# A graph layer's edge attributes copied by group into spare columns of a PSUM tile, and a head in another order

## The chip, the cores and the metric

The kernel runs on one core of a Trainium2 chip. Its engines work side by side, each on its own list of instructions in a fixed order: PE (matrix products into PSUM), DVE (vector work), ACT (scalar functions and copies), POOL (which also issues the gathers) and SP (which only issues DMA). They wait for each other by semaphores. The metric is the device time of one launch in microseconds, the median of several runs. The inputs already lie in device memory.

## The reference

A graph of 1250 nodes with 512 features each (three vector parts of 128, and 128 scalars) and 40,000 edges, sorted by destination. Each edge has a source, a destination, an attribute of three numbers and a weight (its length). One message pass, an update that depends on nodes, a residual and a layer norm:

```python
x_j = x[src]
v_j = x_j[:, :384].reshape(E, 128, 3)
s_j = silu(x_j[:, 384:] @ W1 + b1) @ W3 + b3
edge_basis = rbf * cutoff @ W2 + b2
split = s_j * edge_basis
s1, s2, s3 = split[:, :128], split[:, 128:256], split[:, 256:]
v_msg = v_j * s1[:, :, None] + s3[:, :, None] * edge_attr1[:, None, :]
msg = concatenate([v_msg.reshape(E, 384), s2], axis=1)
x = x + segment_sum(msg, dst)
...
x = layernorm(x0 + x)
```

The left-out part gathers the new rows again, multiplies them with U and V, and adds a second segment sum; the kernel does that by node with counted links instead of by edge.

## The kernel before

**Head.** Everything is loaded, and for every node a row of a table is made: its vector part and `silu(s @ W1 + b1) @ W3 + b3`. `make_rows` does it by blocks of 128 nodes: a product on PE with the bias (L334) and W3 (L335), a copy on ACT (L593), a product on DVE (L594), a store by SP (L599). In between, the destinations `dst_r` become places within a window (`local_r`, L346 on POOL). Two reductions on DVE look for edges that lie outside their window; `misses` (L369) is summed by a one-column product on PE (`missed`, L378), copied to an integer, and decides a branch (L398). `by_tile` turns sources, weights and places into columns by PE transposes (L284). The attributes and places of all edges end up in one SBUF tile, `carried`, of shape 128 x groups x 16 tiles x 4: three attributes and the place. `sh.attr` and `sh.local` are views of it.

**Main loop.** 40,000 edges make 313 tiles of 128. A group g has 16 tiles and a batch t four of them, so t = 4g + i; there are 20 groups, the last one short. A step t of the loop issues, in this order:

- `messages(t)` on DVE: L916 and L918 multiply the gathered rows with the edge factors, which they read from the PSUM tile `eb` (four banks of 512 columns, a tile of edges in each, columns 0 to 383 used); then small work listed under `amid`; then `make_pair` (L939), and for the next batch `make_hot` (L847, a one-hot of the place within the window) and `make_spread` (L859, one-hot times each attribute);
- `add_messages(t-1)` on PE: L955 with the one-hot and L961 with the spread, into the sums by node;
- `count_links(t-1)` on PE: L984, preceded by L976 at a group's first batch;
- work listed under `early`, by step and rank, among it `bring_fades` (L809, a copy of 128x64 on ACT into spare columns of another PSUM tile), `make_basis` and `turn_basis` (L823 on PE, L828 on ACT);
- `edge_factors(t+1)`: L906, four products into `eb` for the next batch;
- `gather(t+3)`: four indirect DMAs on POOL (L756), the first of which also waits for the L906 just issued.

ACT makes a one-hot of sources in two lines, L871 (`distances`) and L881 (`mark_sources`), four instructions each a batch, and every other group a sine (L793). `eb` has a single buffer. Before the change L906 of a batch waits for L918 of the one before, the last that reads `eb`. The dependency is kept by tile: who writes any part of `eb` waits for whoever has read any part of it.

The last three batches use other PSUM tiles, and are not touched.

Of the kernel before, what the change touches and what calls it, by code (L numbers as in the profile page):

```python
# [22 lines left out]
C = 128  # L23
# [41 lines left out]
def gnn_resnorm(  # L65
# [89 lines left out]


    ones = const.tile([P, P], F32)
    nc.vector.memset(ones, 1.0)
# [7 lines left out]

    keep_warm(12)
    bias_f = front.tile([BIAS_ROWS - 1 + 32, V + 2 * C], F32, name="bias_f")
    nc.vector.memset(bias_f, 0.0)
    sh.nodes = const.tile([P, NB * width], F32, name="nodes")  # L170
    sh.xt = sh.nodes.rearrange("p (b f) -> p b f", f=width)
# [3 lines left out]

    inside = SHARE * (NCP - 1) - MARGIN
    assert all(0 <= inside - (SHARE * c - MARGIN) < WIN for c in range(full, NCP))
    dst_r = front.tile([NCP, CHUNK], I32, name="dst_r")
    nc.gpsimd.memset(dst_r[unfilled:, :], inside)
# [3 lines left out]
    nc.gpsimd.memset(sh.src_r[unfilled:, :], 0.0)  # L183

# [7 lines left out]
    def load_inner(engine, cols, b0):  # L192
        load_nodes(engine, sh, sh.xt, b0, min(b0 + 4, NB - 1), cols)
# [6 lines left out]
    load_inner(nc.scalar, of_s, 1)  # L200
    sh.w1_sb = load(nc.sync, w1, [C, C], "w1_sb")
    load_inner(nc.scalar, of_s, 5)
    nc.scalar.activation(warm, warm, AF.Silu)
    for b0 in (1, 5):
        load_inner(nc.gpsimd, slice(0, V), b0)
    load_outer(nc.gpsimd, slice(0, V))
# [139 lines left out]
    nc.gpsimd.tensor_scalar(local_r, dst_r, share, None, op0=ALU.subtract)  # L346
    nc.gpsimd.tensor_scalar(sh.src_r, sh.src_r.bitcast(I32), float(MARGIN), None, op0=ALU.add)
    for i in range(GROUP):
        nc.gpsimd.dma_start(w2_sb[i * FEAT : i * FEAT + N_RBF, :], w2)
        nc.gpsimd.dma_start(  # L350
            w2_sb[i * FEAT + N_RBF : i * FEAT + N_RBF + 1, :], b2.rearrange("(o f) -> o f", o=1)
        )
    ends = front.tile([NCP, 2], F32)
# [5 lines left out]
    inner_layer(next_s, (5, 6, 7, 8))  # L359
    load_edges(sh.wgt_r, edge_weight)  # L360
    make_rows((3, 4))
    nc.vector.tensor_reduce(ends[:, 0:1], local_r, AX.X, ALU.min)
    rest_s = turn_s((0, 9))
    make_rows((5,))
# [6 lines left out]
    )  # L371
    for h in range(2):
        nc.sync.dma_start(
            three[:, V + h * C : V + (h + 1) * C],
            bu2.rearrange("(h o c) -> h o c", o=1, c=C)[2 * h].to_broadcast([3, C]),
        )
    make_rows((7,))
    nc.tensor.matmul(missed, misses, ones[:NCP, 0:1], start=True, stop=True)  # L378
# [7 lines left out]
    part_bias(nc.gpsimd, slice(V, V + 2 * C))  # L386
    load_edges(sh.att_r, edge_attr, 3)
    sh.u_sb = load(nc.sync, u, [C, C], "u_sb")
    sh.v_sb = load(nc.sync, v, [C, C], "v_sb")
# [212 lines left out]
def windowed(tc, sh):  # L602
# [63 lines left out]
    with tc.tile_pool(  # L666
# [163 lines left out]
        def clear_rest(t, tile, engine=nc.vector):  # L830
            g, i = batches[t]
            for j in tiles(g, i):
                m = lanes(g, i, j)
                if m < P:
                    engine.memset(tile[m:, j], 0.0)

        def make_hot(t):
# [15 lines left out]

        def make_spread(t):
            g, i = batches[t]
            for js, n, m in runs(g, i):
                e = i * CPG + js.start
                shape = [m, n, 3, WIN]
                nc.vector.tensor_mul(  # L859
                    spread[t][:m, js],  # L860
                    hots[t][:m, js, None, :].to_broadcast(shape),
                    sh.attr[:m, g, e : e + n, :, None].to_broadcast(shape),
                )
# [1231 lines left out]
```

## Time and profile before

| | |
|---|---|
| runs shown | 568.67, 571.47, 572.39 us; median 571.47 |
| profiled execution | 567.24 us, its span 565.4 us |
| mean granted clock of PE | 0.907 |
| busy on the longest chain (page, part 4) | PE 55%, DVE 20%, ACT 13% |

An instruction's row gives start and duration in us, engine, line, operation, and the tiles it writes and reads. In brackets stands how long the engine was idle before it, and by the trace's inference what ended that. A row "x4" is four instructions in a run, with the time from the first start to the last end. The ends of PE's instructions are modelled. In a stretch's row stand, behind its bounds and length, the busy time of PE, PE's weight loads, DVE, ACT and POOL, then the granted clock of PE, the share of DMA and GB/s.

### The profile page before, as it was taken

To read this page: it belongs to the slowest core of one execution; us is meant where nothing else is said; L and a number is where in the kernel's file an instruction comes from. 1 tells how busy PE (TensorE), PEld (TensorE's weight loads), DVE (VectorE), ACT (ScalarE), POOL (GpSimd) and SP (SyncE) were. 2 spreads that over 40 slices of the span, in tenths; PEclk is the share of its full clock that TensorE was granted. 3 is DMA by queue.
4 is the path that set the end of the run, shared out by engine and by line. 5 is a ranking of instruction groups with operands and counts; after the bars stand their busy time and mean duration, and the time that the engine had idled before them with its cause. 6 is when DMAs were issued, how large, how long until landed. Compare 5 with 4: busy or idle time off the path is not lost.

```text
span 565.4 us, 11226 instructions
## 1 busy us (share of the span) xinstructions
PE 444.6 (79%) x4257; PEld 249.3 (44%) x4257; DVE 432.1 (76%) x660; ACT 377.0 (67%) x955; POOL 350.1 (62%) x377
## 2 busy tenths in 40 slices
PE   8557667677878787767887797879789698989993
PEld 6323233353344344435433443545445354445682
DVE  5576687778877877886778778787878887797675
ACT  3493565567777566775757687577768766788663
POOL 7775666666666666665556665666666666574530
PEclk9856998979897979988788897999989999999997
DMA  8786777777777776776777787678778777877413
GB/s 247 269 243 188 227 228 221 226 214 227 234 222 203 239 223 214 228 230 192 209 217 217 205 258 231 193 234 250 220 237 229 236 224 223 265 217 237 157 56 133
DMA packets 37938, 123.29 MB, mean 218 GB/s; under 512 B 7296, under 2 KB 9870, under 8 KB 37874
## 3 DMA queue, kind: packets, MB, share of 16 engines
q0 software_dynamic: 25824, 104.47, 62.6%
q1 hardware_dynamic: 10850, 17.35, 9.3%
q8 instruction: 35, 0.57, 0.4%
q10 hardware_dynamic: 1200, 0.66, 0.4%
q14 instruction: 29, 0.24, 0.2%
HBM read 112.94 MB, written 9.51 MB: 217 GB/s over the span
## 4 chain that ended last, share of the span: by engine, by line
PE 55%; DVE 20%; ACT 13%; issue 6%; another core or an unknown queue 3%; DMA 2%; POOL 0%; SPq 0%; DVEq 0%; POOLq 0%
PE eb L906 11%; PE agg L955 8%; PE agg L961 6%; DVE more L918 5%; PE adj L984 5%; PE begun L1359 5%; ACT one L881 5%; DVE nodes L918 4%; DVE more L916 3%; PE work L1146 3%; DVE nodes L916 3%; PE work L1051 2%; PE work L823 2%; ACT one L871 2%
## 5 line engine op out<-in xcount | busy, mean ns | idle before, releaser
L756 POOL DMA_INDIRECT more<-table,src_i x189 | 188.8, 999 | 106.2 <-issue 43.0
L756 POOL DMA_INDIRECT nodes<-table,src_i x124 | 123.5, 996 | 68.4 <-issue 28.6
L881 ACT ACTIVATE one<-one,weight,src_f 128x128 f16<-128x128 f16 x313 | 128.6, 483 | 0.2
L916 DVE TENSOR_TENSOR more<-more,eb 128x1024 f32<-128x1024 f32 (+2 forms) x48 | 57.2, 1193 | 63.8 <-PE eb L906 29.9
L871 ACT ACTIVATE one<-number,low 128x128 f16<-128x128 f16 x313 | 99.8, 393 | 6.9 <-remote 4.6
L906 PE MATMUL eb<-w_sb,basis_t 21*128 21x384 f32 x614 | 78.9, 577 | 29.4 <-DVE more L918 14.5
L918 DVE TENSOR_TENSOR more<-more,eb 128x1536 f32<-128x1536 f32 (+2 forms) x48 | 81.8, 1705 | 0.0
L916 DVE TENSOR_TENSOR nodes<-nodes,eb 128x1024 f32<-128x1024 f32 x30 | 36.6, 1222 | 39.4 <-PE eb L906 21.3
L955 PE MATMUL agg<-more,hot 128*32 128x512 f32 x378 | 61.7, 687 | 5.2 <-ACT sums L1006 5.2
L961 PEld LDWEIGHTS agg<-more,spread 128*32 128x32 f32 x1134 | 39.6, 119 | 37.8 <-issue 36.6
L984 PE MATMUL adj<-pair,one 128*128 128x160 f16 x313 | 38.0, 243 | 22.6 <-DVE basis L814 18.7
L918 DVE TENSOR_TENSOR nodes<-nodes,eb 128x1536 f32<-128x1536 f32 x30 | 52.4, 1747 | 0.0
L961 PE MATMUL agg<-more,spread 128*32 128x128 f32 x1134 | 48.6, 291 | 2.7 <-issue 2.7
L906 PEld LDWEIGHTS eb<-w_sb,basis_t 21*128 21x128 f32 x614 | 26.5, 198 | 51.9 <-issue 22.8
L859 DVE TENSOR_TENSOR spread<-hot,carried 128x384 f32<-128x384 f32 (+1 forms) x81 | 44.4, 549 | 2.7
L955 PE MATMUL agg<-nodes,hot 128*32 128x512 f32 x248 | 40.6, 658 | 3.9 <-ACT sums L1006 3.8
L984 PEld LDWEIGHTS <-one 128*128 128x128 f16 x313 | 23.4, 103 | 38.3 <-issue 36.4
L939 DVE TENSOR_TENSOR pair<-number,column 128x640 f16<-128x640 f16 (+1 forms) x81 | 38.7, 479 | 0.0
L961 PEld LDWEIGHTS agg<-nodes,spread 128*32 128x32 f32 x744 | 25.5, 118 | 23.1 <-issue 22.7
L961 PE MATMUL agg<-nodes,spread 128*32 128x128 f32 x744 | 31.8, 289 | 1.0 <-issue 0.9
L828 ACT COPY basis_t<-work 128x512 f32<-128x512 f32 x20 | 11.7, 587 | 29.6 <-PE adj L984 12.3
L1359 PE MATMUL begun<-upper,cast 128*128 128x512 f32 x57 | 28.1, 493 | 0.2 <-ACT cast L1350 0.2
(289 smaller groups left out, 711.2 us busy)
## 6 DMA issues: line engine op xcount, KB each, us to landing
table<-more SPq DMA_DIRECT2D x10, 320.0 KB
more<-table,src_i POOLq DMA_INDIRECT x189
spilled<-begun SPq DMA_DIRECT2D x10, 256.0 KB
more<-spilled SPq DMA_DIRECT2D x2, 1280.0 KB
node_x<-in_x_dram SPq DMA_DIRECT2D x35, 64.0 KB
nodes<-table,src_i POOLq DMA_INDIRECT x124
out_dram<-more SPq DMA_DIRECT2D x7, 256.0 KB
nodes<-in_x_dram POOLq DMA_DIRECT2D x2, 768.0 KB
```

The costliest lines, as they stand in the source:

```text
L756: got = nc.gpsimd.indirect_dma_start(out=rows_t[:n, j, :], out_offset=None, in_=sh.table1, in_offset=bass.IndirectOffsetOnAxis(ap=sh.src_i ...
L859: nc.vector.tensor_mul(spread[t][:m, js], hots[t][:m, js, None, :].to_broadcast(shape), sh.attr[:m, g, e : e + n, :, None].to_broadcast(sh ...
L871: nc.scalar.activation(onehots[t][:, j, :], number[:, :P], AF.Abs, bias=low[:, e : e + 1])
L881: nc.scalar.activation(one, one, AF.Relu, scale=less[:, e : e + 1], bias=worth[:, e : e + 1])
L906: made = nc.tensor.matmul(made_in[t][:, j, :V], turned[g][rows, i, :], sh.w2_sb[rows, :], start=True, stop=True,)
L916: nc.vector.tensor_mul(msg[:m, js, V:], msg[:m, js, V:], factors_of(t, js)[:m, :, C:V])
L918: nc.vector.tensor_mul(msg[:m, js, :V].rearrange("p t (k c) -> p t k c", k=3), msg[:m, js, :V].rearrange("p t (k c) -> p t k c", k=3), fac ...
L939: nc.vector.tensor_tensor(pair[:m, js, :].rearrange("p t (l h) -> p t l h", h=2), number[:m, : PARTS * WIN].rearrange("p (l h) -> p l h", ...
L955: nc.tensor.matmul(agg[j * WIN : (j + 1) * WIN, :], hots[t][:, j, :], msg[:, j, :width], start=(i == 0), stop=False, skip_group_check=True,)
L961: nc.tensor.matmul(agg[j * WIN : (j + 1) * WIN, c * C : (c + 1) * C], spread[t][:, j, c, :], msg[:, j, width:], start=False, stop=(i == la ...
L984: nc.tensor.matmul(to[:, :, at : at + WIN], one[:m, j, :], pair[:m, j, :].rearrange("e (p n) -> e p n", n=WIN), start=(i == 0 and j == js[ ...
L1359: nc.tensor.matmul(acc, casts[a, b], rows[:, a, :], start=(start and a == first and k == 0), stop=(stop and a == end - 1 and k == 1),)
```

## The change

1. `bring_carried(g)`, for the groups 1 to 18: one ACT copy of 128x64 from `carried` to columns 384 to 447 of bank g % 2 of `eb`. It is listed under `early` of step 4g - 3 behind `bring_fades`. `make_hot` and `make_spread` read the copy (groups 0 and 19 still `carried`).
2. In the head: six warming products instead of twelve; W3 is loaded second on SP; `dst` is loaded before SP's node loads; the fill of `dst_r` and the addition of a margin to the sources move from POOL to DVE; the eight loads of W2 and b2 move from POOL to SP, behind the attributes; two loads of bu2 and a bias part come earlier; the misses' product comes behind two more table rows.

```diff
-    keep_warm(12)
+    keep_warm(6)
...
+    sh.w3_sb = load(nc.sync, w3, [C, V], "w3_sb")
...
-    sh.w3_sb = load(nc.sync, w3, [C, V], "w3_sb")
+    load_edges(dst_r, dst)
     load_outer(nc.sync, of_s)
-    load_edges(dst_r, dst)
...
-    nc.gpsimd.tensor_scalar(sh.src_r, sh.src_r.bitcast(I32), float(MARGIN), None, op0=ALU.add)
-    for i in range(GROUP):
-        nc.gpsimd.dma_start(w2_sb[i * FEAT : i * FEAT + N_RBF, :], w2)
...
+    part_bias(nc.gpsimd, slice(V, V + 2 * C))
     make_rows((3, 4))
     nc.vector.tensor_reduce(ends[:, 0:1], local_r, AX.X, ALU.min)
+    nc.vector.tensor_scalar(sh.src_r, sh.src_r.bitcast(I32), float(MARGIN), None, op0=ALU.add)
...
-    make_rows((7,))
+    make_rows((7, 8, 0))
     nc.tensor.matmul(missed, misses, ones[:NCP, 0:1], start=True, stop=True)
-    make_rows((8,))
     nc.vector.tensor_copy(missed_i, missed)
-    make_rows((0, 9))
+    make_rows((9,))
...
     load_edges(sh.att_r, edge_attr, 3)
+    for i in range(GROUP):
+        nc.sync.dma_start(w2_sb[i * FEAT : i * FEAT + N_RBF, :], w2)
...
+        def bring_carried(g):
+
+            to = eb[:, g % 2, V : V + EPG * CARRY].rearrange("p (t k) -> p t k", k=CARRY)
+            nc.scalar.copy(to, sh.carried[:, g])
+            carried_at[g] = to
...
-                    sh.local[:m, g, e : e + n, None].to_broadcast(shape),
+                    carried_of(g)[:m, e : e + n, 3:].to_broadcast(shape),
...
-                    sh.attr[:m, g, e : e + n, :, None].to_broadcast(shape),
+                    carried_of(g)[:m, e : e + n, :3, None].to_broadcast(shape),
...
+        for g in range(1, NGR - 1):
+            at(early, 4 * g - 3, 6.5, bring_carried, g)
```

Line numbers shift: L906 becomes L917, L916 L927, L918 L929, L847 and L859 become L858 and L870, L871 and L881 become L882 and L892, L823 and L828 become L822 and L827, L955 and L961 become L966 and L972, L976 and L984 become L987 and L995. The copy is L841.

PE's rows around the factors of batch 14, before. A row is a line, an operation, the tiles written and read, and in brackets the engines or queues whose semaphores are waited for:

```order
L955 MATMUL agg<-more,hot 32x512 [waits DMASW1_49]
L961 MATMUL agg<-more,spread 32x128 x12
L823 MATMUL work<-ident,basis 128x128 [waits PE_49,Activation_49]
L823 MATMUL work<-ident,basis 128x128 x3
L906 MATMUL eb_403<-w_sb,basis_t 128x384 [waits DVE_49]
L906 MATMUL eb_403<-w_sb,basis_t 128x384 x3
L976 MATMUL adj<-passed,ident 128x5x16 [waits DVE_49]
```

And the same place with the change:

```order
L966 MATMUL agg<-more,hot 32x512 [waits DMASW1_49]
L972 MATMUL agg<-more,spread 32x128 x12
L822 MATMUL work<-ident,basis 128x128 [waits PE_49,Activation_49]
L822 MATMUL work<-ident,basis 128x128 x3
L917 MATMUL eb_397<-w_sb,basis_t 128x384 [waits Activation_49]
L917 MATMUL eb_397<-w_sb,basis_t 128x384 x3
L987 MATMUL adj<-passed,ident 128x5x16
```

The order stays; the factors' first product waited for DVE's L918 and now waits for ACT's copy. This is so for batches 4g - 2. The others wait for DVE as before, but there for `make_spread` (L870) instead of L918.

ACT at the same place, before:

```order
L871 ACTIVATE one<-number,low 128x128 x4
L828 COPY basis_t<-work 128x512 [waits PE_49]
L881 ACTIVATE one<-one,weight,src_f 128x128 [waits Activation_49] x4
L1176 ACT_TABLE_LOAD
L1176 ACTIVATE n_t<-work 128x128 [waits PE_49]
```

And with the change:

```order
L882 ACTIVATE one<-number,low 128x128 x4
L827 COPY basis_t<-work 128x512 [waits PE_49]
L892 ACTIVATE one<-one,weight,src_f 128x128 [waits Activation_49] x4
L841 COPY eb_397<-carried 128x64 [waits DVE_49]
L1187 ACT_TABLE_LOAD
L1187 ACTIVATE n_t<-work 128x128 [waits PE_49]
```

The copy stands behind the basis' copy and four one-hot instructions, and itself waits for DVE's `make_spread`. In the batches 10, 18, ... 66 it stands behind four L892, the sine (L792) and, every other time, `bring_fades` (L808).

PE in the head, where the misses' product moves (L378 before, L374 now), as a piece of the difference:

```order
-L378 MATMUL missed<-ones,misses 1x1 [waits DVE_49]
 L334 LDWEIGHTS ones_r
 L334 MATMUL pp<-bias,ones_r 128x384 [waits Activation_49]
 L335 MATMUL pp<-w_sb,h_t 128x384
 L334 LDWEIGHTS ones_r
-L334 MATMUL pp<-bias,ones_r 128x384
+L334 MATMUL pp<-bias,ones_r 128x384 [waits DVE_49]
 L335 MATMUL pp<-w_sb,h_t 128x384
+L374 MATMUL missed<-ones,misses 1x1 [waits DVE_49]
```

Two table rows that stood behind the product now stand ahead of it.

More of the change, by code (lines that the diff above doesn't have):

```diff
@@ L154, in load @@
         return t
+    inside = SHARE * (NCP - 1) - MARGIN
+    assert all(0 <= inside - (SHARE * c - MARGIN) < WIN for c in range(full, NCP))
     ones = const.tile([P, P], F32)
@@ L165, in keep_warm @@
             nc.tensor.matmul(idle[:, :P], ones, ones, start=True, stop=True)
-    keep_warm(12)
+    keep_warm(6)
     bias_f = front.tile([BIAS_ROWS - 1 + 32, V + 2 * C], F32, name="bias_f")
     nc.vector.memset(bias_f, 0.0)
+    dst_r = front.tile([NCP, CHUNK], I32, name="dst_r")
+    nc.vector.memset(dst_r[unfilled:, :], inside)
     sh.nodes = const.tile([P, NB * width], F32, name="nodes")
@@ L174, in gnn_resnorm @@
     nc.vector.memset(sh.xt[:MARGIN, 0, :], 0.0)
[L176 to L179, printed above, removed]
     diff = front.tile([P, P], I32)
@@ L205, in gnn_resnorm @@
         load_inner(nc.gpsimd, slice(0, V), b0)
+    nc.gpsimd.memset(sh.src_r[unfilled:, :], 0.0)
     load_outer(nc.gpsimd, slice(0, V))
@@ L360, in gnn_resnorm @@
     load_edges(sh.wgt_r, edge_weight)
+    for h in range(2):
+        nc.sync.dma_start(
+            three[:, V + h * C : V + (h + 1) * C],
+            bu2.rearrange("(h o c) -> h o c", o=1, c=C)[2 * h].to_broadcast([3, C]),
+        )
+    part_bias(nc.gpsimd, slice(V, V + 2 * C))
     make_rows((3, 4))
     nc.vector.tensor_reduce(ends[:, 0:1], local_r, AX.X, ALU.min)
+    nc.vector.tensor_scalar(sh.src_r, sh.src_r.bitcast(I32), float(MARGIN), None, op0=ALU.add)
     rest_s = turn_s((0, 9))
@@ L371, in gnn_resnorm @@
     )
[L372 to L376, printed above, removed]
-    make_rows((7,))
+    make_rows((7, 8, 0))
     nc.tensor.matmul(missed, misses, ones[:NCP, 0:1], start=True, stop=True)
-    make_rows((8,))
     nc.vector.tensor_copy(missed_i, missed)
-    make_rows((0, 9))
+    make_rows((9,))
     by_tile(ps_front, sh.src_r, 0, 1, sh.src_f, 1)
@@ L835, in clear_rest, with carried_of @@
                     engine.memset(tile[m:, j], 0.0)
+        carried_at = {}
+        def bring_carried(g):
+            to = eb[:, g % 2, V : V + EPG * CARRY].rearrange("p (t k) -> p t k", k=CARRY)
+            nc.scalar.copy(to, sh.carried[:, g])
+            carried_at[g] = to
+        def carried_of(g):
+            return carried_at.get(g, sh.carried[:, g])
         def make_hot(t):
```

8 lines of the change are left out of this document (3 added, 5 removed).

## The prediction

> **What bounds the kernel now.** I read the page's busy times and costliest groups first, then the timeline of PE, ACT, DVE and POOL around single batches, then the stretches by engine with the granted clock, and the head last. From the page, and from the answer on L756 in the loop (min/median/max in ns):
>
> ```profile
> PE 444.6 (79%) x4257; PEld 249.3 (44%) x4257; DVE 432.1 (76%) x660; ACT 377.0 (67%) x955; POOL 350.1 (62%) x377
> PEclk9856998979897979988788897999989999999997
> L859 DVE TENSOR_TENSOR spread<-hot,carried 128x384 f32<-128x384 f32 (+1 forms) x81 | 44.4, 549 | 2.7
> L756 POOL DMA_INDIRECT more<-table,src_i x189 | 188.8, 999 | 106.2 <-issue 43.0
> L756 POOL DMA_INDIRECT more<-table,src_i x166: 954/960/1296, 59.6 to 479.1; - x166
> ```
>
> No engine is full; the loop is a ring through PE and DVE. A batch t begins with L916 on DVE, which waits for the factors that PE's L906 writes into `eb`; L906 of the next batch in turn waits for L918, the last reader of `eb`. I call the start of L916 the beat. Three batches of the trace, t = 14, 38 and 34, by their timelines (start, duration). First t = 14:
>
> ```profile
> 123.89 0.93 PE L906 MATMUL eb<-w_sb,basis_t 21*128 21x384 f32 x8
> 120.30 1.75 DVE L918 TENSOR_TENSOR nodes<-nodes,eb 128x1536 f32<-128x1536 f32 x1
> 123.81 0.56 DVE L859 TENSOR_TENSOR spread<-hot,carried 128x384 f32<-128x384 f32 x1
> 125.28 1.22 DVE L916 TENSOR_TENSOR nodes<-nodes,eb 128x1024 f32<-128x1024 f32 x1 [0.91 <-PE eb L906]
> ```
>
> Then t = 38, with ACT first, PE, and DVE:
>
> ```profile
> 276.43 0.59 ACT L828 COPY basis_t<-work 128x512 f32<-128x512 f32 x1 [3.14 <-PE adj L984]
> 276.91 1.65 ACT L881 ACTIVATE one<-one,weight,src_f 128x128 f16<-128x128 f16 x4
> ...
> 272.81 0.66 PE L823 MATMUL work<-ident,basis 128*128 128x128 f32 x4
> 273.39 0.93 PE L906 MATMUL eb<-w_sb,basis_t 21*128 21x384 f32 x8
> 277.07 1.65 PE L1146 MATMUL work<-ident,square 128*128 128x128 f32 x6 [1.83 <-ACT basis_t L828]
> ...
> 271.58 1.75 DVE L918 TENSOR_TENSOR more<-more,eb 128x1536 f32<-128x1536 f32 x1
> 275.09 0.56 DVE L859 TENSOR_TENSOR spread<-hot,carried 128x384 f32<-128x384 f32 x1
> 276.52 1.22 DVE L916 TENSOR_TENSOR nodes<-nodes,eb 128x1024 f32<-128x1024 f32 x1 [0.87 <-PE adj L984]
> ```
>
> In t = 38 L918 ends at 273.33, L906 starts at 273.39, yet the beat comes at 276.52: 3.19 us after L918's end. In t = 14 L906 started 1.84 us after L918's end (122.05 to 123.89), and the beat came at 125.28, 3.23 us after it. So the beat doesn't follow L906's start one to one: a start up to about 1.9 us late costs nothing. PE still has earlier work in hand that the modelled ends don't show. In t = 38 ACT, too, gets the result of L823 (modelled end 273.47) only at 276.43.
>
> Last t = 34, ACT, PE, DVE:
>
> ```profile
> 247.37 1.63 ACT L881 ACTIVATE one<-one,weight,src_f 128x128 f16<-128x128 f16 x4
> 248.91 0.72 ACT L793 ACTIVATE turn<-turn 128x640 f32<-128x640 f32 x1
> 249.54 0.20 ACT L809 COPY adj<-fade 128x64 f32<-128x64 f32 x1
> ...
> 246.32 0.93 PE L906 MATMUL eb<-w_sb,basis_t 21*128 21x384 f32 x8
> 249.79 0.72 PE L976 MATMUL adj<-passed,ident 128*128 128x80 f32 x2 [2.54 <-ACT adj L809]
> ...
> 244.00 1.75 DVE L918 TENSOR_TENSOR nodes<-nodes,eb 128x1536 f32<-128x1536 f32 x1
> 248.98 1.22 DVE L916 TENSOR_TENSOR nodes<-nodes,eb 128x1024 f32<-128x1024 f32 x1 [0.40 <-remote]
> ```
>
> **The change, part by part.**
>
> *The new wait on DVE.* L906 (L917 now) waits for the one-hots' spread instead of for L918, since spread now reads a tile in the banks that PE writes. Spread ends at 275.65 in t = 38 and at 124.37 in t = 14, 2.3 us after L918; these two are among the batches with a turn on DVE ahead of it. In a plain batch it comes sooner, as at t = 40:
>
> ```profile
> 284.94 1.75 DVE L918 TENSOR_TENSOR nodes<-nodes,eb 128x1536 f32<-128x1536 f32 x1
> 287.33 0.56 DVE L859 TENSOR_TENSOR spread<-hot,carried 128x384 f32<-128x384 f32 x1
> ```
>
> There spread ends 1.2 us after L918 (286.69 to 287.89). The latest start, 2.3 after, plus 0.93 of L906 and 0.07 to the beat, ends 3.3 us after L918, where 3.2 is usual; the plain one ends at 2.2. I take 0; the cover is PE's unseen work. Without it, each of some 70 batches would lose at least those 1.2 us: bound +84, kept as a rival. Behind L917 on PE stand the sums of the messages, in front of nothing that DVE needs before the next beat.
>
> *The new wait on ACT.* Once in four batches, for t = 4g-2, PE's L917 waits for the copy of group g into `eb` (L841), and that copy stands behind the other work of its step in ACT's queue. Its price is near L809, the nearest row (128x64, 0.20 us, overlapping L793's end by 0.1). So it ends about 0.11 after the instruction ahead of it, and the beat comes 0.05 + 0.93 + 0.07 = 1.05 later.
> In t = 38 the last of four L881 ends at 278.56. Copy 278.67, beat 279.72 instead of 276.52: +3.2. PE's next pieces (L1146 at 277.07) stand behind L917 in its queue and move by as much, so this isn't won back. Eight batches (t = 14, 22, ... 70) look so; t = 6 is milder:
>
> ```profile
> 75.90 1.65 ACT L881 ACTIVATE one<-one,weight,src_f 128x128 f16<-128x128 f16 x4
> 76.17 1.22 DVE L916 TENSOR_TENSOR more<-more,eb 128x1024 f32<-128x1024 f32 x1 [0.75 <-PE adj L984]
> 476.68 1.66 ACT L881 ACTIVATE one<-one,weight,src_f 128x128 f16<-128x128 f16 x4
> 476.29 1.22 DVE L916 TENSOR_TENSOR more<-more,eb 128x1024 f32<-128x1024 f32 x1 [1.19 <-PE eb L906]
> 98.88 0.72 ACT L793 ACTIVATE turn<-turn 128x640 f32<-128x640 f32 x1
> 100.21 1.22 DVE L916 TENSOR_TENSOR more<-more,eb 128x1024 f32<-128x1024 f32 x1 [0.70 <-PE adj L984]
> ```
>
> By these rows t = 70, the last, gives 478.34 + 0.11 + 1.05 - 476.29 = +3.2; t = 6 gives 77.55 + 1.16 - 76.17 = +2.5; t = 10 gives 99.60 + 1.16 - 100.21 = +0.6. Sum of the nine: 8 x 3.2 + 2.5 = 28.1.
> In t = 34 the copy follows L809, which ends at 249.74: beat 250.90 instead of 248.98, +1.9. But there PE's L976 waited for L809 until 249.79 anyway and everything behind it goes on from there; now it starts when L917 ends, near 250.83. So only about 1.1 stays: four such batches (18, 34, 50, 66), 4.4. Three (26, 42, 58) have L793 but no L809, so nothing to give back: 1.8 each, 5.4. With t = 10: 10.4. For t = 2 I take nothing.
> The ends of this term: 28.1 + 10.4 = 38.5 as taken. Lower: L823's result reaches ACT in t = 38 at its modelled end, 3 us sooner, once L906 isn't pressed in behind it; then the copy waits for spread only and the nine batches cost 0.4 each, 14 in all. Upper: L906 costs 1.4 instead of 0.93 after such a wait, +8, 47.
>
> *PE's clock.* PE now idles in 17 places. Stretches by engine, from beat 37 to 38, 38 to 39, 39 to 40 (granted clock behind the busy times):
>
> ```profile
> 270.44:276.52 6.08, 4.61 (x56) 2.71 (x56) 5.17 (x7) 2.31 (x8) 4.10 (x4) 0.99 0.63 185
> 276.52:283.80 7.28, 6.73 (x51) 3.81 (x52) 4.84 (x7) 7.23 (x16) 3.84 (x4) 0.54 0.78 226
> 283.80:289.81 6.01, 5.32 (x70) 2.65 (x73) 4.85 (x7) 3.42 (x10) 3.84 (x4) 1.00 0.65 184
> ```
>
> A batch at half the clock takes 7.28 instead of 6.08 or 6.01: +1.2. The rows also show that a delay isn't made good: the next batch takes 6.01, not less. How many of the 17 places bring a new half-clock batch isn't shown: 0 to 17, so 0 to 20 us. I take 3, 4 us, since slices far below 0.8 are few in the row PEclk now.
> The Trainium skill, "TensorE: Matmul & The Clock Gate", section "HAM oscillation — how this bites in real kernels", says that gaps of PE above about 3.4 us throttle it again. By it the eight long waits, 273.47 to 278.72 on modelled ends, would each bring one: 10 instead of 4, and a sum 6 us higher. The trace only half agrees: its stretch at 0.54 follows a gap of 1.83 us.
>
> *Hot and spread with one operand in PSUM.* L859 costs 44.4 in all; a tenth either way is 4 us on DVE, which waits 0.4 to 1.2 us before each beat shown here. 0.
>
> *The head.* By its timelines:
>
> ```profile
> 14.74 1.57 POOL L346 TENSOR_SCALAR local_r<-dst_r,share 80x512 f32<-80x512 int32 x1 [2.97 <-DMA dst_r<-in_dst_dram]
> 16.19 0.81 PE L335 MATMUL pp<-w_sb,h_t 128*128 128x384 f32 x2
> 19.06 0.19 PE L378 MATMUL missed<-ones,misses 80*1 80x1 f32 x2 [2.07 <-DVE misses L369]
> 13.83 0.30 PE L297 MATMUL xs<-ident,nodes 128*128 128x128 f32 x1 [0.43 <-DMA counts<-in_edge_weight_dram]
> 3.03 1.61 SPq L428 DMA_DIRECT2D nodes<-in_x_dram  x4
> ```
>
> PE stands 2.07 us before the misses' product with three table rows behind it. With the product moved behind two of them that wait goes: at most -2.1. Against it SP issues w3 and dst ahead of the four node loads (1.61 us of issue from 3.03), so L297 at 13.83, which waits for such a load, may come up to 1.5 later. src_r's addition leaves POOL for DVE, which waits there; the eight w2 loads leave POOL for SP behind the attributes and have until L906 of batch 0. bu2's two loads go ahead of table stores on SP, and `part_bias` on POOL goes into what the w2 loads leave free. Fewer warming products: 0, since PE waits for loads behind them. I take -1; ends -2.1 and +1.5.
>
> Sum: 38.5 + 4 - 1 = +41.5. On the profiled run's own 567.24 (span 565.4) that is 608.7. The median of the runs shown, 571.47, lies 4.2 higher; I forecast against it: 613.
>
> **The rivals.**
>
> *ACT is early, the waits shrink.* The lower end above: 14 + 4 - 1 = +17, 588. For it: ACT idles 3.14 us before L828 in t = 38. Against it: it was released there 0.09 before the beat, by work of PE that comes before L906. Chance 0.14.
>
> *Every L917 is late.* If a start after spread moved the beat one to one, +84 on top: 697. t = 14 speaks against it. 0.06.
>
> *Faster: POOL sets the beat.* The gathers' mean is 999 against a minimum of 954 ns; over 313 that is 14 us. If the ring ran through POOL, one operand of hot and spread outside SBUF would give these 14 back, and L917's waits would fall into time in which DVE waits for rows anyway: 571 - 14 - 1 = 556. It decides only if POOL has no idle time, and the page has 106.2 before L756. 0.07. The Trainium skill, "SBUF — State Buffer", section "Who interferes with whom", has it that a DVE instruction with two inputs in SBUF contends with a GpSimd instruction that reads SBUF, and one with a single input doesn't; the spread from 954 to 1296 agrees with some such contention.
>
> *No change.* The copy's wait falls where PE is late anyway in nearly all 17 batches: within 566 to 577. Against it t = 34 and 38, where ACT ends after the beat. 0.07.
>
> **The numbers.** Chances: the forecast 0.66, with 595 to 640 as its own range; ACT early 0.14; all late 0.06; faster 0.07; none 0.07. Low 580 takes in most of the first rival; high 640 takes in 47 for the waits and 20 for the clock. Outside are the last three, 0.20. A measurement of this kernel tells about 1% from no change; slower by more than that: 0.66 + 0.14 + 0.06 = 0.86.
>
> **What would show it.** Right: L917 in every fourth batch released by ACT's L841, and beats 3 us longer there in t = 14, 22, ...; the other beats at about 6.05 (6.08 and 6.01 above). Wrong: L841 ending before the usual beat (ACT early); all beats longer than 7 (all late); beats under 6 (POOL). In the head, the product without a wait and the transposes behind the last table row about a microsecond sooner.

## The result and the profile after

The changed kernel takes 625.34 us in the median (623.36, 624.77, 625.9 and 633.58) against 571.93 for the kernel before (the three runs shown and a fourth, 573.67): 1.093 times as long, with a 95% interval of 1.0862 to 1.0997. This ratio leaves out the 633.58 as a slow run, and those of the experiments leave out runs over 1.5% above the fastest of their kernel. It is slower, inside the predicted range of 580 to 640 and 12 us above the predicted 613. The profiled execution took 623.36 us with a span of 621.5, which is 56.1 more than the span before; PE's mean granted clock fell from 0.907 to 0.861.

From the page of the changed kernel, busy times, the clock in 40 slices, and three of the costliest groups:

```profile
PE 463.2 (75%) x4245; PEld 258.2 (42%) x4245; DVE 432.0 (70%) x662; ACT 378.5 (61%) x973; POOL 330.9 (53%) x367
PEclk8956887878897797988878797979789977889998
L755 POOL DMA_INDIRECT more<-table,src_i x189 | 181.1, 958 | 146.0 <-PE eb L917 86.7
L917 PE MATMUL eb<-w_sb,basis_t 21*128 21x384 f32 x614 | 85.0, 618 | 95.0 <-ACT eb L841 46.9
L870 DVE TENSOR_TENSOR spread<-hot,eb 128x384 f32<-128x384 f32 x72 | 39.9, 554 | 2.5
```

DVE and ACT do as much as before (432.1 and 377.0 then), in a longer time. New is the last figure of L917's row: PE stood still for 46.9 us before the factors, until ACT's copy L841 had come. The gathers on POOL are shorter (958 instead of 999 ns), and wait longer, now mostly for those same factors.

Where the 56 us lie is told by the beats, the distances from one start of L916 (now L927) to the next. Summed over three kinds of batch, from the timelines of the two profiled executions:

| batches | before, us | after, us | difference |
|---|---|---|---|
| t = 6, 14, ... 70 (nine; basis product ahead) | 54.9 | 94.0 | +39.1 |
| t = 10, 18, ... 66 (eight; sine ahead) | 49.0 | 65.9 | +16.9 |
| the other 54 from t = 3 to 73 | 338.6 | 337.1 | -1.5 |
| start of the span up to the beat of t = 2 | 52.15 | 52.81 | +0.7 |

So 56.0 us came in the 17 batches whose factors wait for ACT's copy, and next to nothing elsewhere. Two executions of the same kernel can differ by some 3 us in such a row (below), so the last two differences aren't told from none. One of the nine, t = 14, by its timelines (ACT first, then PE, then DVE):

```profile
130.92 0.59 ACT L827 COPY basis_t<-work 128x512 f32<-128x512 f32 x1 [1.27 <-PE work L822]
131.40 1.65 ACT L892 ACTIVATE one<-one,weight,src_f 128x128 f16<-128x128 f16 x4
132.95 0.20 ACT L841 COPY eb<-carried 128x64 f32<-128x64 f32 x1
...
128.75 0.66 PE L822 MATMUL work<-ident,basis 128*128 128x128 f32 x4
133.21 1.66 PE L917 MATMUL eb<-w_sb,basis_t 21*128 21x384 f32 x8 [3.80 <-ACT eb L841]
...
125.87 1.75 DVE L929 TENSOR_TENSOR nodes<-nodes,eb 128x1536 f32<-128x1536 f32 x1
129.38 0.55 DVE L870 TENSOR_TENSOR spread<-hot,eb 128x384 f32<-128x384 f32 x1
135.00 1.22 DVE L927 TENSOR_TENSOR nodes<-nodes,eb 128x1024 f32<-128x1024 f32 x1 [5.06 <-PE eb L917]
```

The chain reads from the top: the basis's copy, four one-hot instructions, the small copy, and 0.06 us after its end PE's factors; the beat follows 0.13 us after those. DVE had been done with spread since 129.93 and stood 5.06 us. L917 took 1.66 us, where L906 took 0.93.

A batch with the sine and `bring_fades` ahead, t = 34, in the same order:

```profile
269.04 0.72 ACT L792 ACTIVATE turn<-turn 128x640 f32<-128x640 f32 x1
269.66 0.20 ACT L808 COPY adj<-fade 128x64 f32<-128x64 f32 x1
269.80 0.20 ACT L841 COPY eb<-carried 128x64 f32<-128x64 f32 x1
...
270.05 0.93 PE L917 MATMUL eb<-w_sb,basis_t 21*128 21x384 f32 x8 [2.92 <-ACT eb L841]
270.91 0.45 PE L987 MATMUL adj<-passed,ident 128*128 128x80 f32 x2
...
271.11 1.22 DVE L927 TENSOR_TENSOR nodes<-nodes,eb 128x1024 f32<-128x1024 f32 x1 [2.41 <-issue]
```

Here L917 kept its 0.93, and the beat of 8.12 us is 2.0 longer than before (6.12). Last a plain batch, t = 16, DVE ahead of PE:

```profile
142.30 1.75 DVE L929 TENSOR_TENSOR more<-more,eb 128x1536 f32<-128x1536 f32 x1
144.68 0.55 DVE L870 TENSOR_TENSOR spread<-hot,eb 128x384 f32<-128x384 f32 x1
147.27 1.22 DVE L927 TENSOR_TENSOR more<-more,eb 128x1024 f32<-128x1024 f32 x1 [1.22 <-PE work L1206]
...
145.29 0.93 PE L917 MATMUL eb<-w_sb,basis_t 21*128 21x384 f32 x8 [1.78 <-issue]
```

The factors start 1.24 us after L929's end (144.05), and the beat still comes 3.22 us after it, the distance of the kernel before.

### The profile page after: what moved, and what is told of

It is laid out like the page before. It is cut to its first block, busy times and chain, and to the rows that moved or that the text cites. A ratio compares the mean times of both kernels' runs of the same rounds, so it can differ in the third digit from the quotient of the medians.

```text
span 621.5 us, 11228 instructions
## 1 busy us (share of the span) xinstructions
PE 463.2 (75%) x4245; PEld 258.2 (42%) x4245; DVE 432.0 (70%) x662; ACT 378.5 (61%) x973; POOL 330.9 (53%) x367
## 4 chain that ended last, share of the span: by engine, by line
PE 55%; DVE 18%; ACT 14%; issue 6%; another core or an unknown queue 2%; SPq 0%; DMA 0%; POOL 0%; DVEq 0%; POOLq 0%; ACTq 0%
PE eb L917 16%; PE agg L966 9%; ACT one L892 6%; PE agg L972 5%; DVE more L929 5%; PE adj L995 4%; DVE more L927 4%; PE begun L1370 4%; DVE nodes L929 3%; PE work L1157 3%; DVE nodes L927 2%; PE work L822 2%; ACT one L882 2%; PE work L1062 2%
## 5 line engine op out<-in xcount | busy, mean ns | idle before, releaser
L755 POOL DMA_INDIRECT more<-table,src_i x189 | 181.1, 958 | 146.0 <-PE eb L917 86.7
L755 POOL DMA_INDIRECT nodes<-table,src_i x124 | 118.5, 956 | 96.8 <-PE eb L917 55.5
L917 PE MATMUL eb<-w_sb,basis_t 21*128 21x384 f32 x614 | 85.0, 618 | 95.0 <-ACT eb L841 46.9
L892 ACT ACTIVATE one<-one,weight,src_f 128x128 f16<-128x128 f16 x313 | 128.5, 482 | 0.2
L927 DVE TENSOR_TENSOR more<-more,eb 128x1024 f32<-128x1024 f32 (+2 forms) x48 | 57.2, 1193 | 102.0 <-PE eb L917 75.4
L882 ACT ACTIVATE one<-number,low 128x128 f16<-128x128 f16 x313 | 99.8, 392 | 24.5 <-PE adj L995 17.4
L929 DVE TENSOR_TENSOR more<-more,eb 128x1536 f32<-128x1536 f32 (+2 forms) x48 | 81.8, 1705 | 0.0
L927 DVE TENSOR_TENSOR nodes<-nodes,eb 128x1024 f32<-128x1024 f32 x30 | 36.6, 1221 | 58.2 <-PE eb L917 38.8
L917 PEld LDWEIGHTS eb<-w_sb,basis_t 21*128 21x128 f32 x614 | 27.4, 205 | 117.4 <-ACT eb L841 50.7
L966 PE MATMUL agg<-more,hot 128*32 128x512 f32 x378 | 66.3, 725 | 1.0 <-ACT sums L1017 0.6
L972 PEld LDWEIGHTS agg<-more,spread 128*32 128x32 f32 x1134 | 41.4, 123 | 35.4 <-issue 34.1
L929 DVE TENSOR_TENSOR nodes<-nodes,eb 128x1536 f32<-128x1536 f32 x30 | 52.4, 1747 | 0.0
L995 PE MATMUL adj<-pair,one 128*128 128x160 f16 x313 | 39.4, 252 | 16.9 <-DVE basis L813 16.9
L972 PE MATMUL agg<-more,spread 128*32 128x128 f32 x1134 | 49.3, 299 | 0.0
L966 PE MATMUL agg<-nodes,hot 128*32 128x512 f32 x248 | 41.9, 711 | 0.9 <-ACT sums L1017 0.6
L870 DVE TENSOR_TENSOR spread<-hot,eb 128x384 f32<-128x384 f32 x72 | 39.9, 554 | 2.5
L995 PEld LDWEIGHTS <-one 128*128 128x128 f16 x313 | 25.7, 109 | 33.8 <-issue 33.2
L972 PEld LDWEIGHTS agg<-nodes,spread 128*32 128x32 f32 x744 | 26.2, 121 | 23.4 <-issue 22.5
L972 PE MATMUL agg<-nodes,spread 128*32 128x128 f32 x744 | 31.2, 294 | 0.0
L1370 PE MATMUL begun<-upper,cast 128*128 128x512 f32 x57 | 30.1, 529 | 0.0
L1062 PE MATMUL work<-sums,sel 128*128 128x512 f32 x36 | 29.3, 939 | 0.2
```

Of the source, the lines that this page charges most:

```text
L755: got = nc.gpsimd.indirect_dma_start(out=rows_t[:n, j, :], out_offset=None, in_=sh.table1, in_offset=bass.IndirectOffsetOnAxis(ap=sh.src_i ...
L870: nc.vector.tensor_mul(spread[t][:m, js], hots[t][:m, js, None, :].to_broadcast(shape), carried_of(g)[:m, e : e + n, :3, None].to_broadcas ...
L882: nc.scalar.activation(onehots[t][:, j, :], number[:, :P], AF.Abs, bias=low[:, e : e + 1])
L892: nc.scalar.activation(one, one, AF.Relu, scale=less[:, e : e + 1], bias=worth[:, e : e + 1])
L917: made = nc.tensor.matmul(made_in[t][:, j, :V], turned[g][rows, i, :], sh.w2_sb[rows, :], start=True, stop=True,)
L927: nc.vector.tensor_mul(msg[:m, js, V:], msg[:m, js, V:], factors_of(t, js)[:m, :, C:V])
```

## Experiments

The theories. **A**, mine: the copy, late in ACT's queue, holds PE's L917 in 17 batches. Against it: L917's later start behind spread costs in every batch; the slow factors come from PE's clock after its pauses (**D**); the head loses time because the rows' bias (b3) arrives behind W3's load (**F**); or the reads and writes in PSUM themselves cost (**B**, together with the wait for spread). The experiments fell on four chips. On two of them the kernel before takes 567 to 571 us, as in the result; on the other two 494 to 496. So each ratio is against the kernel before on the same chip.

Beats of all profiled executions, summed as in the table above, with the median of the 54 others. Each row is one execution; two rows of one kernel show the scatter:

| kernel | nine, us | eight, us | 54 others, us | median |
|---|---|---|---|---|
| before | 54.9 | 49.0 | 338.6 | 6.10 |
| before, another chip | 57.8 | 49.9 | 338.4 | 6.19 |
| after | 94.0 | 65.9 | 337.1 | 6.17 |
| change of the loop alone | 91.4 | 66.4 | 335.0 | 6.09 |
| change of the head alone | 56.0 | 51.6 | 332.7 | 6.11 |
| copy first in its step | 65.3 | 52.5 | 338.4 | 6.09 |
| copy first, another chip | 65.3 | 50.6 | 343.3 | 6.17 |
| copy into SBUF | 56.7 | 51.7 | 335.6 | 6.11 |
| *faster chips:* before | 48.9 | 45.5 | 278.1 | 4.99 |
| W3 behind b3, loop as after | 67.4 | 55.0 | 301.5 | 5.43 |
| copy made, unread | 65.4 | 49.4 | 290.6 | 5.01 |
| copy made, unread, another chip | 63.4 | 49.3 | 290.4 | 5.02 |
| copy by DVE | 61.1 | 47.6 | 295.2 | 5.33 |
| PE kept at work | 61.4 | 51.0 | 291.5 | 5.13 |

**The loop alone and the head alone.** The first adds `bring_carried`, `carried_of` and the schedule's line to the kernel before; the second takes them out of the changed one.

```diff
 # main_only, on the kernel before
-                    sh.local[:m, g, e : e + n, None].to_broadcast(shape),
+                    carried_of(g)[:m, e : e + n, 3:].to_broadcast(shape),
...
+            at(early, 4 * g - 3, 6.5, bring_carried, g)
 # head_only, on the changed kernel
...
-            at(early, 4 * g - 3, 6.5, bring_carried, g)
```

> The kernel before with the copies of the main loop alone; the head is as before. Theory A (PE waits in every fourth batch for a copy that stands late in ACT's queue): the main loop carries nearly everything, 618 to 630 us, with beats of about 10.2 us at t = 14, 22, 30 and 8.1 at t = 18, 34. Rival H (a part comes from the head, whose table rows begin 3.5 us later in the changed kernel): under 616 us.

> The changed head alone, without copies. Theory A: within 1% of the kernel before, 568 to 577 us: the table rows begin 3.5 us later, end 0.9 later, and the main loop is as before. Rival H: 580 us or more.

Measured: 617.43 and 568.05 us against 566.63, which is 1.09 (1.0827 to 1.0973) and 1.0019 (0.9975 to 1.0063). The first lies just under A's 618 to 630, with the beats as expected. The loop's part carries all of it, the head nothing that can be told from no change.

**The copy first in its step.** The same copy, from ACT, ahead of the basis's copy and the one-hots.

```diff
-            at(early, 4 * g - 3, 6.5, bring_carried, g)
+            at(early, 4 * g - 3, -2, bring_carried, g)
```

> The changed kernel, but the copy is issued first among the work of its step, so on ACT it stands ahead of the basis' copy and the four one-hot instructions. It writes the same place and PE waits for it as before. Theory A: 576 to 590 us; the beats of the batches 4g-2 fall from 10.2 and 8.1 to 6.1 to 7.2 us. Rival B (what costs is that L917 waits for spread at all, or that DVE reads the attributes from PSUM): it stays above 610 us.

Measured: 576.28 us, 1.0163 (1.0096 to 1.0231). Some four fifths of the loss are gone: 9.7 us are left (576.28 - 566.63) of the loop's 50.8. (The profiled execution, which the table shows, was its longest, 583.29.) Twelve of the 17 beats lie at 6.1 to 7.2 us as expected; t = 6, 26, 54, 62 and 70 take 7.35 to 8.19. Batch 14 by its timelines, ACT, PE, DVE:

```profile
126.83 0.22 ACT L841 COPY eb<-carried 128x64 f32<-128x64 f32 x1 [1.09 <-DVE spread L870]
127.68 0.59 ACT L827 COPY basis_t<-work 128x512 f32<-128x512 f32 x1 [0.64 <-PE work L822]
...
126.75 0.89 PE L822 MATMUL work<-ident,basis 128*128 128x128 f32 x4
127.57 0.93 PE L917 MATMUL eb<-w_sb,basis_t 21*128 21x384 f32 x8
...
126.24 0.56 DVE L870 TENSOR_TENSOR spread<-hot,eb 128x384 f32<-128x384 f32 x1
128.62 1.22 DVE L927 TENSOR_TENSOR nodes<-nodes,eb 128x1024 f32<-128x1024 f32 x1 [1.83 <-PE eb L917]
```

The copy now waits for spread alone and is done at 127.05, half a microsecond before L917, which no longer stands. A second run on the other of these two chips, where the kernel before takes 570.81, scattered: 576.11 in one run and 585.75 to 587.53 in three, too wide for an interval; how much of the loss is left there stays open. The ratio on a faster chip, which this run was also to tell, wasn't measured.

> The same kernel as copy_first. Theory P: on a chip where the kernel before takes about 567 us, 1.01 to 1.025 times as long as before, as then; on a chip where it takes about 494 us, 1.04 to 1.07 times, since nothing of PE covers the wait for spread there. Rival Q: the same ratio on both.

**The copy into SBUF.** As many ACT copies at the same place, into a tile of its own.

```diff
-            to = eb[:, g % 2, V : V + EPG * CARRY].rearrange("p (t k) -> p t k", k=CARRY)
+            to = pool.tile([P, EPG, CARRY], F32, name="carried_g", bufs=2)
```

> The changed kernel, but the copy goes to an SBUF tile of its own (two buffers) at the same place in ACT's queue, so that PE waits neither for it nor for spread. Theory A: 568 to 577 us. Rival C (18 more instructions on ACT push its other work back): 590 us or more.

Measured: 568.69 us, 0.9995 (0.9945 to 1.0046). The copy's time on ACT costs nothing; its place in `eb`, with the waits of PE for the copy and for spread that come with it, costs everything. Its page also shows the gathers on POOL when both operands of hot and spread are in SBUF again:

```profile
L755 POOL DMA_INDIRECT more<-table,src_i x189 | 186.9, 989 | 107.9 <-issue 42.7
```

The gathers are back at 989 ns, where the changed kernel has 958 and the kernel with the copy first, which also reads PSUM, 959. The changed head alone has 988, so a part of the 41 ns came with the head.

**Copies made and not read; the copy by DVE.** The first leaves the one-hots and spread on `carried`, so L917 waits for the copy and for L929, but for no spread. The second puts the copy first and gives it to DVE.

```diff
 # unread
...
-                    carried_of(g)[:m, e : e + n, :3, None].to_broadcast(shape),
+                    sh.attr[:m, g, e : e + n, :, None].to_broadcast(shape),
 # copy_dve, beside rank -2
-            nc.scalar.copy(to, sh.carried[:, g])
+            nc.vector.tensor_copy(to, sh.carried[:, g])
```

> The changed kernel with its copies, but nobody reads them: hot and spread read SBUF as before. PE still waits for the copy in the batches 4g-2, and for L929 instead of spread in the others. Theory A (the queue on ACT): 612 to 628 us, the beats at t = 14, 22, 30 stay near 10.2 and those at 18, 34 near 8.1; against the changed kernel only the other beats shrink, by 0.05 to 0.1 us each, 3 to 5 us in all. Rival B (the wait for spread or the reads from PSUM cost): under 605 us.

> The changed kernel, but DVE makes the copy itself, right behind spread; PE waits for DVE alone. Theory A: 567 to 580 us, the beats of the batches 4g-2 under 7 us, since the copy is done 0.2 us after spread. Rival B: above 600 us, since all batches wait for spread and the reads from PSUM stay.

Measured, on a chip where the kernel before takes 494.27: 524.14 us, 1.051 (1.0427 to 1.0593), and 527.21, 1.0634 (1.0544 to 1.0724). The unread copy was run once more, on the other fast chip: 524.34 against 495.85, 1.061 (1.0511 to 1.071).

> The same kernel as unread, whose copies nobody reads. On a chip where the kernel before takes about 567 us, theory A: 1.08 to 1.10 times before, 612 to 626 us, beats near 10.2 at t = 14, 22, 30 and 8.1 at 18, 34, since only the wait for ACT is left; rival B (the wait for spread or the reads from PSUM cost a good part): under 1.06. On a chip where before takes about 494 us: 1.04 to 1.06 as in the first run of it.

The copy's wait alone, with nothing read from it, costs 16.5 us in the nine batches (65.4 against 48.9; the second run, on the same chip as that 48.9, has 63.4, or 14.5 more), which is A again. With the copy by DVE ACT is out of it, and yet 12.2 us remain in the nine: the copy stands behind spread on DVE, and L917 behind the copy. The expected times were worked out from the slower chips. Put as ratios to 566.63, A's ranges (1.08 to 1.11 for the unread copy, 1.00 to 1.02 for the copy by DVE) miss both, and the second run of the unread copy lies just above its 1.04 to 1.06. With the unread copy it is A's own price that is lower on these chips (see the rivals below). The copy by DVE lies in B's range (over 1.06): it costs 32.9 us without ACT. And with everything read, as in the changed kernel, the one execution below took 543.36, some 19 more than the unread copy. So on the faster chips A isn't the whole: the wait for spread or the reads from PSUM cost there too, and which of the two isn't shown.

**PE kept at work, and W3 behind b3.** The first puts two products that nobody reads ahead of L917 in the batches 6, 14, ... 70, so that PE's pause is shorter. The second is the changed kernel with W3's load behind b3's; its loop is that of the changed kernel, and stands for it on this chip, with one execution only.

```diff
 # stay_warm
+        def stay_warm():
+            idle = work()
+            for _ in range(2):
+                nc.tensor.matmul(idle[:, :V], ident, sh.w2_sb, start=True, stop=True)
...
+        for g in range(2, NGR - 1, 2):
+            at(early, 4 * g - 3, 6.6, stay_warm)
 # w3_behind
-    sh.w3_sb = load(nc.sync, w3, [C, V], "w3_sb")
...
     nc.sync.dma_start(three[:, :V], b3.rearrange("(o f) -> o f", o=1).to_broadcast([3, V]))
+    sh.w3_sb = load(nc.sync, w3, [C, V], "w3_sb")
```

> The changed kernel with two idle products of 384 columns on PE ahead of L917 in the batches 8k+6, into the basis' PSUM tile; their result is not read. Theory D (L917 takes 1.66 instead of 0.93 us there because PE has stood idle and got half the clock): L917 falls to about 0.93, the nine beats from 10.2 to 9.5, 6 us in all, 615 to 621. Rival E (the length of L917 there has another cause, or so short a stretch of work doesn't bring the clock back): L917 stays at 1.66 and the time at 622 to 630.

> The changed kernel with W3 loaded behind b3 again. Theory F (b3's bias comes late because W3's load went ahead of it): the first table row begins near 9.5 instead of 12.3 us and the transposes behind the last row 1 to 3 us sooner than 23.7. Rival G (the small b3 load is slow for other reasons, dst and the node loads): still above 11.5 us. The whole time is the same within 1% of the changed kernel.

Measured: 526.93 us for the first, 1.0654 (1.0577 to 1.0731), and 543.36 in a single run for the second, both against 494.27. Batch 14 with PE kept at work, ACT and then PE:

```profile
115.67 0.57 ACT L827 COPY basis_t<-work 128x512 f32<-128x512 f32 x1
117.68 0.22 ACT L846 COPY eb<-carried 128x64 f32<-128x64 f32 x1
...
114.88 0.66 PE L822 MATMUL work<-ident,basis 128*128 128x128 f32 x4
116.30 1.56 PE L839 MATMUL work<-w_sb,ident 128*128 128x384 f32 x4 [0.76 <-ACT basis_t L827]
117.95 0.93 PE L922 MATMUL eb<-w_sb,basis_t 21*128 21x384 f32 x8
```

And the same batch's factors, with W3 behind b3:

```profile
116.22 1.60 PE L917 MATMUL eb<-w_sb,basis_t 21*128 21x384 f32 x8 [2.42 <-ACT eb L841]
```

Both start 2.66 us after L929's end, so the copy's wait is the same; but after the two idle products the factors take 0.93 us, in this and the other eight batches, without them 1.60 here and 0.97 to 1.67 in the others. In the beats of the loop (t = 0 to 73) the idle products save 19.9 us: 6.0 in the nine batches, 4.0 in the eight, 10.0 in the others, head apart. The 6.0 is what D had named; what the idle products do for the batches that have none isn't shown, and the 19.9 is one execution against one. So D holds for the nine, on top of A: the pause that the copy makes also costs clock, though not always in L917. The unread copy has the same pause before batch 14, and there L917 keeps 0.93, while products behind it are slow: eight L966 take 1.63 us, and 1.06 with PE kept at work (L971 there).

```profile
113.63 0.93 PE L917 MATMUL eb<-w_sb,basis_t 21*128 21x384 f32 x8 [2.42 <-ACT eb L841]
116.89 1.63 PE L966 MATMUL agg<-nodes,hot 128*32 128x512 f32 x8
```

With PE kept at work the wait remains, and the kernel stays behind the one before.

For F the first bias product of the table, and the first transpose behind the table, with W3 behind b3:

```profile
10.73 0.48 PE L334 MATMUL pp<-bias,ones_r 65*128 65x384 bf16 x1 [3.09 <-DVE bias L321]
...
22.14 0.44 PE L284 MATMUL tp<-ident,counts 80*128 80x80 f32 x4
```

With PE kept at work, on the same chip and with W3 ahead, they stand at 12.66 and 25.01. F is right in direction, 1.9 and 2.9 us, but W3's place is the small part of b3's delay. In the kernel before SP issues b3's load at 1.71 us, and DVE's first use of it, L316, starts at 4.94. The changed kernel has 2.15 and 8.70. With W3 behind b3 the issue is at 1.71 again, and still:

```profile
7.97 0.44 DVE L316 CAST bias<-bias_f 65x384 bf16<-65x384 f32 x1 [2.56 <-DMA bias_f<-in_L_gnn_b_dram]
```

Only 0.7 of the 3.8 us come back. The other 3.0 have another cause, which is G's reason, though 10.73 falls between F's 9.5 and G's 11.5. `dst`'s load, now issued at 3.03 ahead of the node loads, is a candidate that no run tried.

**The kernel before, twice more**, for the difference between chips.

> The kernel before, unchanged, profiled on the chip of this call. Theory P (on some chips PE needs longer than its modelled ends say, and that sets the ring of 6.05 us): if the time is near 567 us, L916 starts 1 to 2 us after L906's modelled end in plain batches; if it is near 494 us, within 0.5 us, and the beats lie between 4.3 and 5.8 us and follow PE's work. Rival Q (the fast runs differ in something else, as the gathers): the distance from L906's modelled end to L916 is the same in both.

> The kernel before, unchanged, for its profile on the chip of this call. Theory P as for before_again: near 567 us L916 starts 1 to 2 us after L906's modelled end in plain batches; near 494 us within 0.5 us, with beats between 4.3 and 5.8 us.

Measured: 568.21 us where other runs of it had a median of 570.81, and 492.34 where they had 495.85. Batch 9 on the faster chip, PE and then DVE:

```profile
79.86 0.93 PE L906 MATMUL eb<-w_sb,basis_t 21*128 21x384 f32 x8 [0.80 <-DVE nodes L918]
...
78.06 1.75 DVE L918 TENSOR_TENSOR nodes<-nodes,eb 128x1536 f32<-128x1536 f32 x1
82.14 1.22 DVE L916 TENSOR_TENSOR nodes<-nodes,eb 128x1024 f32<-128x1024 f32 x1 [1.14 <-DMA nodes<-table,src_i]
```

From L918's end (79.81) to the beat it is 2.33 us here; on the slower chips some 3.2. Over the 54 other batches the beat comes 0.79 us (median) after L906's modelled end here, and 1.59 in the run on the slower chip. P had named 0.5 at most here and 1 to 2 there, so it is right in direction and for the slower chip; Q, the same distance on both, isn't what was found. In the batch shown DVE waits for gathered rows, not for PE, so the 0.79 isn't all PE's. What makes PE's results later on the slower chips stays open.

## Why the prediction was right, and where not

**Direction and mechanism: right.** The likeliest case was L917 waiting for ACT's L841 in 17 batches. The 56.0 us lie in just these batches, the loop alone carries them, and the copy put first takes most of them away. Chance 0.86 had been given to slower.

**The wait on ACT: right mechanism, term too small.** 38.5 was taken, up to 47; it measured 56.0. Three things make the 17.5.
- L917's length: the sum kept 0.93 and had 1.4 only as its upper end. It took 1.66 in seven of the 17 and 1.44 and 1.14 in two more: 7 x 0.73 + 0.51 + 0.21 = 5.8.
- The give-back of 0.8 in the four batches with `bring_fades` didn't come: t = 18, 34 and 50 grew by 1.99, 2.00 and 2.10, and the beats behind t = 18 and 66 changed by -0.01 and +1.02. That is 3.2. (Those behind 34 and 50 are shorter by 1.97 and 0.96, but t = 35 ran at 0.58 and t = 50 at 0.54 before.)
- The rest is 8.5, for the sum took the copy's place from the kernel before, and what stands ahead of it moved too. (Where it didn't, in t = 14, 22 and 30, the beats grew by 4.1: the forecast 3.2, L917's 0.73, and 0.2.) The largest is t = 70, whose beat grew by 5.69 instead of 3.2, and 2.5 of the rest with it: there PE had waited 2.28 us for ACT's L1134 (1.11 before), its products behind that wait ran slowly (1.94 us for eight L966, before 1.06), and the basis's product came late.

```profile
521.29 1.65 PE L1141 MATMUL work<-uv,x_t 128*128 128x128 f32 x6 [2.28 <-ACT vu L1134]
...
527.85 0.59 ACT L827 COPY basis_t<-work 128x512 f32<-128x512 f32 x1 [2.85 <-PE work L822]
```

The other 6.0 lie mostly in t = 6, 46, 54, 58, 62 and 66, with 0.6 to 0.9 each, and stay open.

**The wait on DVE: right here.** 0 was taken, against a bound of +84. The other 54 batches are 1.5 us shorter in all, though L917 starts later in them, as t = 16 shows. That the run fell on such a chip is luck, for the prediction knew of no other. On the faster chips this cover is thinner: with the loop of the changed kernel their 54 batches take 23.4 more (301.5 against 278.1). Spread isn't the only cause, since the unread copy takes 12.5 more there without that wait, and PE kept at work 13.4 with it. How it divides stays open.

**The clock: about the size, in another place.** 4 was taken for batches newly at half the clock. None came. By stretches from beat to beat, six batches ran at 0.54 to 0.58 before (t = 23, 28, 35, 39, 44, 50), and none of t = 3 to 73 below 0.65 after. Some beats grew behind a wait (t = 59 by 1.71, at 0.70), former half-clock batches shrank (t = 35 by 1.97), and the other batches net lost nothing; the cost sits within the waits, in L917's 5.8 above. That it comes near the 4 is luck. The stretches by engine, from beat 13 to 14 and from there to 0.06 us before beat 15 (clock behind the busy times), show it:

```profile
124.73:135.00 10.27, 4.96 (x51) 2.74 (x52) 5.17 (x8) 8.40 (x21) 4.09 (x4) 0.83 0.56 165
135.00:141.10 6.10, 6.10 (x59) 4.01 (x60) 4.76 (x7) 3.64 (x10) 3.79 (x4) 0.72 0.67 179
```

The batch behind the pause ran at 0.72, with PE busy all through by its modelled ends, and its beat still took 6.16: here such a dip cost the beat nothing (t = 67, also at 0.72, grew by 1.02). The prediction's price of 1.2 was for 0.54, and had nothing to apply to. The Trainium skill, "TensorE: Matmul & The Clock Gate", section "HAM oscillation — how this bites in real kernels", puts the limit for PE's gaps at about 3.4 us. The rows agree in part: 1.66 after modelled gaps of 3.80 (t = 14) and 4.81 (t = 30), 0.93 after 2.92 (t = 34); but with a gap of 2.42 it is 1.60 with W3 behind b3 and 0.93 with the unread copy, and t = 46 has this row:

```profile
353.43 1.66 PE L917 MATMUL eb<-w_sb,basis_t 21*128 21x384 f32 x8 [2.33 <-ACT eb L841]
```

A modelled gap alone doesn't decide it in these runs.

**Hot and spread with an operand in PSUM: right.** 554 ns instead of 549 for spread; 0 on DVE.

**The head: wrong step, small.** -1 was taken, +0.7 measured at the beat of t = 2. The misses' product lost its wait, as said, but the sum looked at SP's order only for the node loads. b3's load, and the rows' bias with it, also comes later, and W3's load ahead of it makes only 0.7 us of that (above). Before and after:

```profile
4.94 0.35 DVE L316 CAST bias<-bias_f 65x384 bf16<-65x384 f32 x1 [0.25 <-DMA bias_f<-in_L_gnn_b_dram]
```

```profile
8.70 0.47 DVE L316 CAST bias<-bias_f 65x384 bf16<-65x384 f32 x1 [3.28 <-DMA bias_f<-in_L_gnn_b_dram]
...
12.30 0.48 PE L334 MATMUL pp<-bias,ones_r 65*128 65x384 bf16 x1 [5.24 <-DVE bias L321]
22.77 0.19 PE L374 MATMUL missed<-ones,misses 80*1 80x1 f32 x2
23.72 0.44 PE L284 MATMUL tp<-ident,counts 80*128 80x80 f32 x4
```

The table starts at 12.30 instead of 8.78, and the transposes behind it at 23.72 instead of 22.82, where a gain of one microsecond had been named as the sign of being right. The first beat is 3.5 us later (40.42 against 36.94), that of t = 2 only 0.7, for the kernel before took 9.09 us from beat 1 to beat 2 there, the changed one 6.23. In the second profile of the kernel before on a slower chip the beat of t = 2 comes at 49.22 instead of 52.15, so the 0.7 is no firm figure. The firm one is the head alone, 1.0019.

**The rivals.** ACT is early (588): no; in t = 14 ACT still stood 1.27 us for the basis's product, and the copy ended at 133.15, 2.3 us after the usual time of the beat (3.2 behind L929's end at 127.62). The prediction's reason against it was misread, though: L984, which ACT's L828 was released by in t = 38, stands behind L906 there (274.79 and 273.39 us), since in these steps the links are counted behind the factors. And on the faster chips this rival came about: with W3 behind b3, ACT's copy of the basis begins 0.19 to 1.28 us behind L929's end in the nine batches, where the changed kernel on the slower chip has 3.15 to 5.59, and the nine cost 18.5 us (67.4 - 48.9) instead of 39.1. Every L917 late (697): no. POOL sets the beat (556): no. The gathers did get shorter, 312.3 us to 299.6 over both their tiles, and POOL's idle time before L755 rose from 106.2 to 146.0. The Trainium skill, "SBUF — State Buffer", section "Who interferes with whom", has it that a DVE instruction with at most one input in SBUF, outside its 2-port modes, doesn't contend with GpSimd. The traces agree in the main: 988 ns with the head alone and 989 with the copies in SBUF, 958 and 959 with an input in PSUM. But the unread copy, with both inputs in SBUF, has 972 on a faster chip, where the kernel before has 995, so something else shortens them too. POOL isn't on the path here. No change: it is what the copy into SBUF gives.

No version tried is faster than the kernel before. The head alone and the copy into SBUF equal it.

## What to carry to other kernels

Spare columns of a PSUM tile aren't free storage where dependencies are kept by tile: whoever writes the tile next waits for the copy and for its readers, and a 0.2 us copy at the end of another engine's queue made most beats of every fourth batch 2 to 4 us longer. Price such a wait from the whole queue ahead of the copy, add what a pause does to PE's clock in the instructions behind it, and look first whether the copy can stand early in its queue or outside the tile. When loads change places, look at when each of the others lands, too: here a small one that was issued at the same time as before came 3 us later.

## What the runs showed of the hardware

The same kernel takes 567 to 571 us on two chips and 494 to 496 on two others, each time in several runs. In the trace the difference shows as the time at which others see PE's results. In the kernel before, over the nine batches, ACT's copy of the basis began 1.17 to 3.34 us after the modelled end of PE's product on a slower chip, and 0.04 to 0.98 us after it on a faster one. In t = 14 ACT's copy of the basis began 0.13 us after the modelled end of PE's product on a faster chip (115.54 to 115.67, with PE kept at work, right behind other work of ACT), and 1.51 us after it on a slower one (129.41 to 130.92, the changed kernel), where ACT was already idle. The mean granted clocks differ less: 0.938 and 0.907 in the two profiled executions of the kernel before. The modelled ends alone don't tell which kind of chip a trace is from.
